# Layer 1 of a two-layer attention block: keys, queries and landmarks of all head pairs first, then each pair's iteration beside two other pairs

## The chip, the cores and the metric

The kernel runs on one core of one Trainium2 chip. The core has a matrix engine (TensorE, PE in the profile; its weight loads are listed apart as PEld), three engines for element-wise work (VectorE or DVE, ScalarE or ACT, GpSimd or POOL), and queues for DMAs, of which this kernel uses that of SyncE (SP) for nearly all and POOL's for a few. The metric is the device time of one execution in microseconds (us). Everything is computed in fp32; each fp32 matmul of the program appears in the profile as two instructions.

## What is computed

The input x has 2 batch items of 512 channels and 64 x 32 = 2048 tokens. There are two layers; both have 8 heads of 64 channels, which the kernel takes two at a time as a "pair", so a batch item has 4 pairs.

Layer 0 is a full softmax attention over 2048 tokens, with an embedding added to keys and queries, an output projection, and the residual.

Layer 1 is a Nyström attention on the normalised tokens xn, and after it a linear feed-forward on the normalised sum:

```
q, k, v = split(xn @ Wqkv);  q = q / 8
qL, kL  = mean of q and of k over each run of 8 tokens       # 256 landmarks
attn1 = softmax(q  @ kL.T)      # 2048 x 256
attn2 = softmax(qL @ kL.T)      # 256 x 256
attn3 = softmax(qL @ k.T)       # 256 x 2048
out   = attn1 @ (pinv(attn2) @ (attn3 @ v)) + conv(v)   # 33 taps along the tokens
t     = t + out @ Wout + bout
t     = t + (norm(t) @ w_lora.T) @ W.T
```

pinv is 6 steps of an iteration that starts from attn2.T divided by (largest row sum times largest column sum) over all heads and both batch items. So every landmark matrix has to exist before the first iteration can start.

## The kernel before

Everything is one program for one core. PE, DVE, ACT and POOL run their instructions in the order in which the Python code emits them; DMA issues on SP are placed by the framework's scheduler, which may put them ahead of their place in the code as soon as the buffer is free. Matmuls write PSUM, which has 8 banks of 128 x 512 fp32. A helper such as `bank` (line 723) hands out a buffer of a pool with a tag; a tag with n buffers is handed out in turn, and who gets one waits until the last user of that buffer is through.

Interleaving is written by hand with generators. A generator emits a unit of work up to each `yield`; `advance(gens, n)` (line 765) takes n units from a list of generators. So "beside" means: units of one thing are emitted between steps of another, on the same engines.

PSUM in before: tag `pp` with 2 banks (`bank`), tag `sc` with 2 double banks (`scores_bank`, 128 x 2 x 512), and `av0`, `av1` with one bank each, which `values_bank` hands out alternately.

The order of the work:

- Layer 0: `attention0` (line 1030) for each of 8 pairs, with the projections of the next pair beside it. Beside the last of them (batch item 1, pair 3) run `landmarks_beside(0)` (line 1244), which computes landmarks and attn2 of batch item 0 from token sums of xn that the normalisation has stored, and keys and values of layer 1's first pair.
- The output projection and normalisation of batch item 1 (`out0`, `norm0_steps`, from line 1805), with attn3, queries and convolution of layer 1's first pair beside them.
- `landmarks_staged` (line 1268): landmarks, attn2 and its Gram matrix for the 4 pairs of batch item 1. `Landmarks.project` (line 1178) multiplies the pooled tokens by the weights (line 1183), `attend` (line 1192) makes attn2, `gram` (line 1221) its product with itself. `start_scale` (line 1297) reduces the scale.
- For each of 8 pairs, batch item 0 first (line 1850): attn3 and queries, `iteration_start`, convolution, then `pinv` (line 1533), then `attn1` (line 1614) with the values of the next pair beside it. Keys of the next pair come at the end of `pinv`. The output part of batch item 0 (`finish1_units`, line 1716) is the only filler inside `pinv`, from the fifth pair on.
- The output part of batch item 1 at the end.

The iteration works on symmetric 256 x 256 matrices M[h] and R[h] of both heads h, with 64 more columns for the vectors. `square` (line 1544) multiplies a matrix by itself in two blocks, `flip` (line 1527) transposes one block into its mirror place: a PE transpose into PSUM and an ACT copy back. One step of the iteration is: `square(M[h])` for both heads (PE tile `pa`), DVE combinations (line 1553), `square(R[h])` for both heads (`pb`), DVE combinations again.

Of the kernel before, what the change touches and what calls it, by code (L numbers as in the profile page):

```python
# [10 lines left out]
F32 = mybir.dt.float32  # L11
# [5 lines left out]
P = 128  # L17
# [5 lines left out]
TB = 512  # L23
# [638 lines left out]
def fast_path(  # L662
# [32 lines left out]

    nc = tc.nc
# [3 lines left out]
    ps = ctx.enter_context(tc.tile_pool(name="ps1", bufs=2, space=bass.MemoryType.PSUM))  # L700
# [12 lines left out]
    pooled_d = dram.tile([B, P, KC, LM], F32, name="pooled_fd")  # L713
    mT_d = dram.tile([P, KC, C], F32, name="mT_fd")
    X_d = dram.tile([B, NPAIR, P, 4, LM], F32, name="X_fd")
# [13 lines left out]
    def values_bank(name):  # L729

        i = values_bank.made % 2
        values_bank.made += 1
        return ps.tile([P, 512], F32, tag=f"av{i}", name=name, bufs=1)

    values_bank.made = 0
# [233 lines left out]
    def norm0_steps(b, t, xb, xn, part, pooled=None):  # L969


        toks = slice(t * TB, (t + 1) * TB)
        name = f"n0_{b}_{t}"
        squares = lambda: (xb[:, :2, :], xb[:, 2:, :])
        for rstd in statistics(xb, xn, part, name, squares, lambda: deviation(name)):
            yield
        nc.vector.reciprocal(rstd, rstd)
        wide = rstd.unsqueeze(1).to_broadcast([P, 2, TB])
        other = nc.vector if t == NTB - 1 else nc.gpsimd
        other.tensor_tensor(xn[:, 2:, :], xn[:, 2:, :], wide, ALU.mult)  # L980
        nc.vector.tensor_tensor(xn[:, :2, :], xn[:, :2, :], wide, ALU.mult)
        nc.gpsimd.dma_start(chunked(xh_d[b])[:, :, toks], xn)
        yield
        n = TB // POOL
        landmarks = slice(t * n, (t + 1) * n)
        if pooled is None:
            pl = small.tile([P, KC, n], F32, tag="pl", name=f"pl_{name}", bufs=1)
            parts = [(pl, xn)]
        else:
            parts = [(pooled[i][:, :, landmarks], xn[:, 2 * i : 2 * i + 2, :]) for i in range(2)]  # L990
        for to, of in parts:
            nc.vector.tensor_reduce(to, of.rearrange("p k (m l) -> p k m l", l=POOL), AX.X, ALU.add)
        if pooled is None:
            nc.sync.dma_start(pooled_d[b][:, :, landmarks], pl)
        yield
# [3 lines left out]
    def finish0_units(b, oTs, outs_done):  # L999
        last = None  # L1000
        for t in range(NTB):
# [10 lines left out]
            if last:  # L1012
                yield from gap()
                next(last)
# [11 lines left out]
        next(last)  # L1026
        yield from gap(2)
# [136 lines left out]
    def load_w(w, hp, n):  # L1164
        for j in range(n):
            lo = j * HEADS * D + hp * P
            nc.sync.dma_start(w[:, :, j, :], chunked(wqkv[:, lo : lo + P]))

    class Landmarks:

        def __init__(self, b, hp, pooled, w, X):
            self.b, self.hp, self.i = b, hp, b * NPAIR + hp
            self.pooled, self.w, self.X = pooled, w, X
            load_w(w, hp, 2)

        def project(self):
            L = row_of(f"L_{self.i}").rearrange("p (j m) -> p j m", j=2)
            lp = bank(f"lp_{self.i}")  # L1180
            for j in range(2):
                for k in range(KC):
                    nc.tensor.matmul(
                        lp[:, j * LM : (j + 1) * LM], lhsT=self.w[:, k, j, :], rhs=self.pooled[k // 2][:, k % 2, :],
                        start=k == 0, stop=k == KC - 1,
                    )
            for j in range(2):
                nc.scalar.mul(L[:, j, :], lp[:, j * LM : (j + 1) * LM], (D**-0.5 if j == 0 else 1.0) / POOL)
            nc.sync.dma_start(L_d[self.b, self.hp], L)
            self.L = L  # L1190

        def attend(self):
            i, L = self.i, self.L
            X = self.X = self.X()
            rs = small.tile([P, 4], F32, tag="rs2", name=f"rs2_{i}")
            for h in range(2):
                nc.gpsimd.memset(X[h][:, :, LM:], 1.0)
            for h in range(2):
                rows_h = slice(h * D, (h + 1) * D)
                sc = bank(f"sc2_{i}_{h}")  # L1200
                for t in range(2):
                    nc.tensor.matmul(
                        sc[:, t * LM : (t + 1) * LM],
                        lhsT=L[rows_h, 0, t * P : (t + 1) * P],
                        rhs=L[rows_h, 1, :],
                        start=True,
                        stop=True,
                    )
                nc.scalar.activation(X[h][:, :, :LM], sc.rearrange("p (t n) -> p t n", n=LM), AF.Exp)
            for h in range(2):  # L1210
                two = slice(2 * h, 2 * h + 2)
                x_h = X[h][:, :, :LM]
                nc.vector.tensor_reduce(rs[:, two], x_h, AX.X, ALU.add)
                nc.vector.reciprocal(rs[:, two], rs[:, two])
                nc.vector.tensor_tensor(
                    x_h, x_h, rs[:, two].unsqueeze(2).to_broadcast([P, 2, LM]), ALU.mult
                )
                nc.sync.dma_start(X_d[self.b, self.hp][:, two], x_h)
                nc.vector.tensor_reduce(rsum[:, i, two], x_h, AX.X, ALU.add)

        def gram(self, h):

            i, X = self.i, self.X
            a = zpool.tile([P, 2, LM + D], F32, tag=f"R{h}", name=f"A0_{i}_{h}")
            for t in range(2):
                pr = bank(f"pr_{i}_{h}_{t}")
                cols = slice(t * P, LM + 1)
                for k in range(2):
                    nc.tensor.matmul(
                        pr[:, cols],  # L1230
                        lhsT=X[h][:, k, t * P : (t + 1) * P],
                        rhs=X[h][:, k, cols],
                        start=k == 0,
                        stop=k == 1,
                    )
                nc.scalar.copy(a[:, t, cols], pr[:, cols])
                nc.sync.dma_start(A_d[self.b, self.hp, h][:, t, t * P :], a[:, t, t * P : LM])
            nc.vector.tensor_copy(csum[:, i, 2 * h : 2 * h + 2], a[:, :, LM])

    def pooled_tiles(b):  # L1240
        tiles = [zpool.tile([P, 2, LM + D], F32, tag=f"M{i}", name=f"pooled_{b}_{i}") for i in range(2)]
        return [tile[:, :, :LM] for tile in tiles]

    def landmarks_beside(b):

        pooled = pooled_tiles(b)
        for i in range(2):
            nc.sync.dma_start(pooled[i], pooled_d[b][:, 2 * i : 2 * i + 2])
        for hp in range(NPAIR):
            w = wpool1.tile([P, KC, 3, P], F32, tag="w", name=f"wL_{b}_{hp}")  # L1250
            lm = Landmarks(
                b, hp, pooled, w,
                lambda: [
# [789 lines left out]
```

## Time and profile before

| | |
|---|---|
| median of 3 runs | 2875.84 us (2872.44 to 2879.71) |
| the profiled execution's own time | 2879.97 us |
| its span, first to last instruction | 2878.2 us |
| PE busy | 2787.5 us (97%) |
| DVE busy | 1746.6 us (61%) |
| ACT busy | 870.6 us (30%) |
| POOL busy | 262.5 us (9%) |
| DMA | 103.59 MB, mean 36 GB/s |

Times inside the span count from its start. Layer 0's attention ends near 1460 us, the landmarks of batch item 1 near 1640 us, and the eight iterations with their surroundings near 2750 us. "Busy" of PE is modelled: ends of matmuls are not observed, so a busy PE isn't necessarily at its peak. The clock column of a stretch is the mean share of full TensorE clock that was granted in it. A row of the table of groups has the line, the engine, the operation, output and inputs, the shape, the count, then busy time and mean duration of one in ns, then the idle time of the engine before these instructions and what ended it.

### The profile page before, as it was taken

To read this page: it belongs to the slowest core of one execution; us is meant where nothing else is said; L and a number is where in the kernel's file an instruction comes from. 1 tells how busy PE (TensorE), PEld (TensorE's weight loads), DVE (VectorE), ACT (ScalarE), POOL (GpSimd) and SP (SyncE) were. 2 spreads that over 40 slices of the span, in tenths; PEclk is the share of its full clock that TensorE was granted. 3 is DMA by queue.
4 is the path that set the end of the run, shared out by engine and by line. 5 is a ranking of instruction groups with operands and counts; after the bars stand their busy time and mean duration, and the time that the engine had idled before them with its cause. 6 is when DMAs were issued, how large, how long until landed. Compare 5 with 4: busy or idle time off the path is not lost. (4 is left out here: it accounts for less than half of the span.)

```text
span 2878.2 us, 39302 instructions
## 1 busy us (share of the span) xinstructions
PE 2787.5 (97%) x16834; PEld 1384.1 (48%) x16834; DVE 1746.6 (61%) x1955; ACT 870.6 (30%) x1158; POOL 262.5 (9%) x160
## 2 busy tenths in 40 slices
PE   8999999999999999999999999999999988999999
PEld 4343443434343343344444756566656534565633
DVE  3869788765667857657558364535445544454475
ACT  1344434433243344444331221212121301222110
POOL 1101011010101100100002010101010100001010
PEclk9999999999999999999999999999999999999999
DMA  3000000101012100022024200002000010000021
GB/s 114 1 5 1 5 1 1 60 15 45 27 47 73 51 1 1 1 79 79 28 74 167 87 14 17 17 20 83 6 23 32 17 53 34 10 19 13 1 72 47
DMA packets 78152, 103.59 MB, mean 36 GB/s; under 512 B 8320, under 2 KB 48016, under 8 KB 77712
## 3 DMA queue, kind: packets, MB, share of 16 engines
q1 hardware_dynamic: 73472, 84.16, 9.1%
q0 software_dynamic: 4416, 16.79, 1.5%
q8 instruction: 134, 2.20, 0.3%
q14 instruction: 50, 0.41, 0.0%
q10 hardware_dynamic: 80, 0.03, 0.0%
HBM read 64.13 MB, written 36.84 MB: 35 GB/s over the span
## 5 line engine op out<-in xcount | busy, mean ns | idle before, releaser
L1060 DVE TENSOR_TENSOR acc_f<-acc_f,p_f 128x1024 f32<-128x1024 f32 x448 | 609.9, 1361 | 239.6 <-ACT p_f L1050 211.3
L1050 ACT ACTIVATE p_f<-sc_f 128x1024 f32<-128x1024 f32 x512 | 497.0, 1022 | 574.0 <-PE sc_f L1042 566.5
L1042 PE MATMUL sc_f<-q_f,k_f 64*64 64x512 f32 x4096 | 494.2, 598 | 3.3 <-ACT p_f L1050 3.3
L1072 PE MATMUL av_f<-p_f,v_f 64*64 64x512 f32 x4096 | 484.0, 589 | 0.0
L1072 PEld LDWEIGHTS av_f<-p_f,v_f 64*64 64x64 f32 x4096 | 156.6, 133 | 282.9 <-issue 282.9
L1042 PEld LDWEIGHTS sc_f<-q_f,k_f 64*64 64x64 f32 x4096 | 144.2, 133 | 292.0 <-issue 251.6
L1329 PE MATMUL pp<-xh,w 128*128 128x512 f32 x512 | 234.2, 603 | 5.8 <-ACT q L1335 2.3
L1540 PE MATMUL pa<-M 128*128 128x192 f32 (+1 forms) x640 | 156.9, 381 | 0.0
L1645 POOL TENSOR_TENSOR o<-o,rinv 128x512 f32<-128x512 f32 x32 | 58.3, 1821 | 1028.2 <-DVE rinv L1643 1025.5
L1540 PE MATMUL pb<-R 128*128 128x192 f32 (+1 forms) x640 | 151.2, 379 | 0.0
L1329 PEld LDWEIGHTS pp<-xh,w 128*128 128x128 f32 x512 | 93.5, 191 | 117.4 <-issue 102.4
L1091 POOL TENSOR_TENSOR q_f<-q_f,rinv_f 128x512 f32<-128x512 f32 x32 | 67.5, 2109 | 850.1 <-DVE rinv_f L1090 850.1
L1642 DVE RECIPROCAL rinv<-rs 128x512 f32<-128x512 f32 x32 | 107.4, 3356 | 56.2 <-PE rs L1638 56.2
L909 PEld LDWEIGHTS vp<-w,xh 128*128 128x128 f32 x1024 | 118.4, 194 | 25.8 <-ACT p L1610 14.6
L909 PE MATMUL vp<-w,xh 128*128 128x128 f32 x1024 | 124.0, 280 | 3.3 <-ACT R L1516 3.3
L1540 PEld LDWEIGHTS pb<-R 128*128 128x128 f32 x640 | 113.9, 193 | 25.5 <-issue 0.5
L1540 PEld LDWEIGHTS pa<-M 128*128 128x128 f32 x640 | 111.5, 196 | 25.0 <-issue 2.0
L909 PEld LDWEIGHTS vp_f<-wv_f,x 128*128 128x128 f32 x1024 | 115.6, 192 | 12.7 <-issue 10.2
L924 PE MATMUL yp_f<-q_f,wo_f 128*128 128x512 f32 x256 | 118.8, 619 | 2.4 <-DVE rinv_f L1090 2.4
L864 PE MATMUL pp_q_f<-x,wq_f 128*128 128x512 f32 x256 | 118.4, 616 | 1.1 <-DVE ft_q_f L850 0.7
L909 PE MATMUL vp_f<-wv_f,x 128*128 128x128 f32 x1024 | 118.5, 276 | 0.0
L924 PE MATMUL yp_g<-o,wo_f 128*128 128x512 f32 x256 | 113.4, 596 | 4.0 <-DVE xb_g L931 2.2
(193 smaller groups left out, 2973.6 us busy)
## 6 DMA issues: line engine op xcount, KB each, us to landing
x<-in_x_dram SPq DMA_DIRECT2D x8, 1024.0 KB, 5.3
xr_f<-in_x_dram SPq DMA_DIRECT2D x8, 1024.0 KB, 5.0
x_fd<-xr_f POOLq DMA_DIRECT2D x8, 1024.0 KB, 4.7
xh_fd<-xn_f POOLq DMA_DIRECT2D x8, 1024.0 KB, 4.6
xh<-xh_fd SPq DMA_DIRECT2D x8, 1024.0 KB, 5.0
xb_g<-x_fd SPq DMA_DIRECT2D x32, 256.0 KB, 4.6
out_dram<-xb_g SPq DMA_DIRECT2D x32, 256.0 KB, 2.3
w<-in_wqkv_dram SPq DMA_DIRECT2D x24, 256.0 KB, 3.7
```

The costliest lines, as they stand in the source:

```text
L864: nc.tensor.matmul(pp, lhsT=w_sb[kind][:, k, cols], rhs=xbs[t][:, k, :], start=k == 0, stop=k == KC - 1)
L909: nc.tensor.matmul(vp[:, j * P : (j + 1) * P], lhsT=xb[:, k, j * P : (j + 1) * P], rhs=w_of(k), start=k == 0, stop=k == KC - 1,)
L924: nc.tensor.matmul(yp, lhsT=wo_sb[:, k, m * P : (m + 1) * P], rhs=oTs[k][:, toks], start=k == 0, stop=k == NPAIR - 1,)
L1042: nc.tensor.matmul(sc[r * D : (r + 1) * D, h, :], lhsT=hd.k[rows, lo : lo + D], rhs=hd.q[rows, t * TB : (t + 1) * TB], start=True, stop=True,)
L1050: nc.scalar.activation(p, sc, AF.Exp, scale=D**-0.5)
L1060: nc.vector.tensor_tensor(acc, first if c == 1 else acc, p, ALU.add)
L1072: nc.tensor.matmul(av[r][half, :], lhsT=hd.v[keys, c, half], rhs=pp[keys, h, :], start=c == 0, stop=c == NST - 1,)
L1091: nc.gpsimd.tensor_tensor(o, o, rinv, ALU.mult)
L1329: nc.tensor.matmul(pp, lhsT=self.w[:, k, j, :], rhs=self.xhs[t][:, k, :], start=k == 0, stop=k == KC - 1)
L1540: nc.tensor.matmul(dst, lhsT=lhsT[:, k, t * P : (t + 1) * P], rhs=rhs[:, k, :], start=k == 0, stop=k == 1)
L1642: nc.vector.reciprocal(rinv, rs)
L1645: nc.gpsimd.tensor_tensor(o, o, rinv, ALU.add)
```

## The change

Landmarks no longer come from pooled tokens. All keys and queries of layer 1 are computed first, pair after pair; each projection unit copies its bank with ACT, stores the piece to a DRAM buffer (`k_d`, `q_d`), and DVE reduces it to landmarks and to its largest magnitude. `attend` and `gram` of a pair run as its `front`, beside the projection of the next pair. Later each pair's keys and queries are read back from DRAM.

Then the iterations run, batch item 1 first. Between the steps of `pinv` of pair n there are 17 places called `slot()`. Each takes one unit of attn1 of pair n-1 (`before`) and one unit of `second(n + 1)` (`nexts`): values 4, attn3 5, landmark values 2, start values 2, convolution 4 units; from the fifth pair on also a unit of the output part of batch item 1 in every other slot. Two units of attn1 come ahead of the first slot.

PSUM is handed out anew after the projections: tag `pp` 3 banks, `pr` 2 banks (products of the iteration, one bank each instead of two), `av0` (all flips), `av1` (attn1's values), `av3` (attn3's values). Attention scores of attn1 and attn3 therefore go to two single `pp` banks with two ACT exponentials of 512 columns, where before they went to one double bank with one exponential of 1024. The scaling of M by the start scale moves from POOL to DVE. Outputs of two pairs are parked in DRAM (`o_d`). The pooled sums in `norm0_steps` and the class `Landmarks` with its projection go.

The core of the diff:

```diff
+    def side_bank(i, name):
         return ps.tile([P, 512], F32, tag=f"av{i}", name=name, bufs=1)
+    def product_bank(name):
+        return ps.tile([P, 512], F32, tag="pr", name=name, bufs=2)
...
+        def keys_and_queries(self, pool, tag, xhs, after=lambda t: None):
...
+            for t in range(NTB):
+                toks, marks = slice(t * TB, (t + 1) * TB), slice(t * TB // POOL, (t + 1) * TB // POOL)
+                for j, dst, dst_d in ((1, k, k_d), (0, q, q_d)):
+                    pp = bank(f"pp{j}_{self.name}_{t}")
+                    for c in range(KC):
+                        nc.tensor.matmul(
+                            pp, lhsT=self.w[j][:, c, :], rhs=xhs[t][:, c, :], start=c == 0, stop=c == KC - 1
+                        )
+                    nc.scalar.copy(dst[:, toks], pp)
+                    nc.sync.dma_start(dst_d[self.b, self.hp][:, toks], dst[:, toks])
+                    nc.vector.tensor_reduce(
+                        self.L[j][:, marks], dst[:, toks].rearrange("p (m l) -> p m l", l=POOL), AX.X, ALU.add
+                    )
+                    nc.vector.tensor_reduce(
+                        big[:, j, t : t + 1], dst[:, toks], AX.X, ALU.max, apply_absolute_value=True
+                    )
+                    if t == NTB - 1:
+                        L = self.L[j]
+                        nc.vector.tensor_scalar(L, L, (1.0, D**-0.5)[j == 0] / POOL, None, ALU.mult)
+                        nc.sync.dma_start(L_d[self.b, self.hp][:, j, :], L)
+                    yield
...
+        def front(self):
+            self.attend()
+            yield 3
             for h in range(2):
+                self.gram(h)
+                yield 0
...
         def attn3(self):
...
+                scs = [bank(f"sc3_{self.name}_{s}_{h}") for h in range(2)]
...
+                for h in range(2):
+                    nc.scalar.activation(p[:, h, :], scs[h], AF.Exp)
...
         def landmarks_values(self):
...
+            rinv = self.acc3[0]
+            yT = rinv[:, LM:]
+            nc.vector.reciprocal(rinv[:, :LM], rs[:, :LM])
+            nc.vector.tensor_tensor(yT, self.av3[:, :LM], rinv[:, :LM], ALU.mult)
+            yield
+            tp = bank(f"tp_{self.name}")
+            for t in range(2):
+                nc.tensor.transpose(tp[:, t * P : (t + 1) * P], yT[:, t * P : (t + 1) * P], ident)
...
         def flip(self, X, name):
-            tp = values_bank(f"tp_{name}_{self.name}")
+            tp = side_bank(0, f"tp_{name}_{self.name}")
             nc.tensor.transpose(tp[:, :P], X[:, 0, P:LM], ident)
             nc.scalar.copy(X[:, 1, :P], tp[:, :P])
...
+            self.flip(M[0], "M0")
+            flip = M[1], "M1"
             for it in range(PINV_ITERS - 1):
                 for h in range(2):
                     pr = square(M[h], f"pa_{it}_{h}_{self.name}", flip)
...
-                advance(gens, n_fill)
+                slot()
                 for h in range(2):
                     pr = square(R[h], f"pb_{it}_{h}_{self.name}", flip)
...
-                advance(gens, n_fill)
+                slot()
                 self.flip(M[0], f"M0_{it}")
                 flip = M[1], f"M1_{it}"
+            slot()
             self.flip(*flip)
...
+                self.product_transposed(wide, src, M, f"{i}")
+                slot()
+                tp = self.into_rows(wide, side_bank(0, f"tp_{i}_{self.name}"))
...
+                slot()
...
+        def attn1(self):
             for t in range(NTB):
...
+                    scs = [bank(f"sc1_{self.name}_{t}_{j}_{h}") for h in range(2)]
...
+                    for h, sc in enumerate(scs):
+                        nc.scalar.activation(p[:, h, :], sc, AF.Exp, scale=D**-0.5)
                     yield
+                acc = apool.tile([P, 2, 512], F32, tag="acc", name=f"acc1_{self.name}_{t}")
+                nc.vector.tensor_tensor(acc, *ps_, ALU.add)
+                av = side_bank(1, f"av1_{self.name}_{t}")
...
+                yield
                 rs = bank(f"rs1_{self.name}_{t}")
...
                 nc.vector.reciprocal(rinv, rs)
+                nc.vector.tensor_tensor(rinv, av, rinv, ALU.mult)
+                nc.gpsimd.tensor_tensor(self.o[:, toks], self.o[:, toks], rinv, ALU.add)
+                yield
...
+    def beside(main, other):
+        for n in main:
+            yield
+            for _ in range(n):
+                if next(other, other) is other:
+                    break
+                yield
...
+    banks.close()
+    ps = ctx.enter_context(tc.tile_pool(name="ps2", bufs=3, space=bass.MemoryType.PSUM))
...
+    def slot():
+        nonlocal made
+        advance(before)
+        advance(nexts)
+        made += 1
+        if finish and (made % 2 or n == len(todo) - 1):
+            advance(finish)
...
+    for n, pair in enumerate(todo):
+        if n + 1 < len(todo):
+            todo[n + 1].prefetch()
+            nexts.append(second(n + 1))
...
+        pair.iteration_start()
         if n:
+            advance(before, 2)
...
+        pair.pinv(slot)
+        while before or nexts:
+            advance(before)
+            advance(nexts)
+        before.append(pair.attn1())
```

## The prediction

> **What bounds the kernel now.** I read the page's busy times, then the table by stretch for where PE is not full, then the groups by shape for what a piece costs, then the chain of waits inside an iteration, then the timeline at the widest hole.
>
> ```profile
> span 2878.2 us, 39302 instructions
> PE 2787.5 (97%) x16834; PEld 1384.1 (48%) x16834; DVE 1746.6 (61%) x1955; ACT 870.6 (30%) x1158; POOL 262.5 (9%) x160
> ```
>
> PE carries the kernel, so only two things can change the time: the sum of PE's work, and holes in it. The table by stretch (length; busy PE, PEld, DVE, ACT, POOL with counts; PE clock; DMA share, GB/s) shows the holes: the staged landmarks of batch item 1, an ordinary iteration with its surroundings, and the output part of batch item 0 where no other work was left.
>
> ```profile
> 1560.00:1640.00 80.00, 71.78 (x377) 51.94 (x376) 42.84 (x66) 19.77 (x44) 8.01 (x16) 0.93 0.37 123
> 1874.20:2004.80 130.60, 128.98 (x722) 79.53 (x724) 63.42 (x99) 30.33 (x55) 11.98 (x8) 1.00 0.13 41
> 2300.00:2420.00 120.00, 97.53 (x296) 43.25 (x294) 49.74 (x54) 10.20 (x15) 0.00 (x0) 0.89 0.15 51
> ```
>
> An iteration has 1.6 us of holes in 130.6. The chain of waits (start, length, what) shows why:
>
> ```profile
> 1894.17 2.81 PE pb L1540 x12
> 1901.87 2.81 PE pb L1540 x12
> 1909.57 2.81 PE pb L1540 x12
> ```
>
> One step of `pinv` follows the other every 7.7 us with no filler at all, and the chain stays on PE. Putting other work between the steps has next to nothing to cover.
>
> ```profile
> L1183 PE MATMUL lp<-pooled,wL 128*128 128x256 f32 x128 | 31.0, 399 | 1.2 <-ACT X L1209 1.2
> L1642 DVE RECIPROCAL rinv<-rs 128x512 f32<-128x512 f32 x32 | 107.4, 3356 | 56.2 <-PE rs L1638 56.2
> L1466 DVE RECIPROCAL acc<-rs 128x256 f32<-128x256 f32 x8 | 14.0, 1756 | 5.2 <-PE rs L1457 5.2
> L1420 ACT ACTIVATE p<-sc 128x1024 f32<-128x1024 f32 x64 | 62.4, 1024 | 87.8 <-PE sc L1412 86.1 <-DVE acc L1440 1.6 <-ACT p L1420 0.2
> L1209 ACT ACTIVATE X<-sc 128x512 f32<-128x512 f32 x16 | 9.0, 597 | 7.5 <-issue 3.4 <-PE sc L1202 3.4 <-DMA wL<-in_wqkv_dram 0.5
> ```
>
> These five rows are prices: a removed projection, the two slow DVE operations, and exponentials of 1024 and 512 columns. The timeline at 2348 us prices a hole:
>
> ```profile
> 2347.87 1.12 PE L946 MATMUL mean_g<-xn_g,mean_w 128*128 128x512 f32 x2 [2.83 <-DVE xn_g L943]
> 2355.12 2.05 PE L959 MATMUL var_g<-sq_g,mean_w 128*128 128x512 f32 x2 [6.13 <-DVE sq_g L956]
> ```
>
> Two matmuls of one size take 1.12 us here, and 2.05 after 6 us of idleness.
>
> **What the Trainium skill says.** "TensorE: Matmul & The Clock Gate", Part 1: the clock falls to half after an idle window of some 3.4 us, a window that runs freely. The trace agrees, by the two rows above and the clock column (0.89 at 2300:2420); holes near 2 us are often enough. "TensorE: Matmul & The Clock Gate", Part 2: matmuls stay in program order, only weight loads are pulled ahead, so one waiting matmul holds all behind it. At 2378.80 PE stood 1.45 us for a bank that DVE had not read, with 16 matmuls ready behind. "ScalarE: Activation LUTs", What ACT_TABLE_LOAD costs: about 0.19 us fixed and 0.83 ns per element; for 512 and 1024 columns 0.61 and 1.04, measured 0.597 and 1.024. So two half exponentials cost 1.19 for 1.02.
>
> **What goes.** (1) Landmark projections: 31.0 us of PE (L1183); all else PE does is still done. (2) Staged landmarks: 80 - 71.8 = 8 us of holes and 0.07 x 80 = 6 of clock, 14. Their matmuls move beside projections. (3) The bare output part: 120 - 97.5 = 22.5, plus about half of the clock deficit of 13 (the rest falls into the holes), less 2 that is ordinary: 27. (4) The iterations' own holes, 8 x 1.6 = 13, which the waits below replace. Sum 85.
>
> **What comes at no cost.** ACT takes all projection copies (0.59 us per unit of 3.44 of PE), DVE two reductions (0.69 each by L1219's shape, 1.4 per unit); PE's unit hides both, uncovered they would be 2 us in each of 64 units. M's scaling moves to DVE (six short operations, about 1.5 us by L1137's 0.42 for 512 columns) behind two attn1 units of 2.1 us. Stores and reloads of k and q (33.6 MB), xn again (4.2) and parked outputs (4.2) add 42 MB to 104, in a kernel whose DMA share in an iteration is 0.06 to 0.13; weights have three buffers, and the landmark, key and query reloads have an iteration's lead.
>
> **What comes at a cost, and what is late next.**
>
> A. `attend` is emitted straight after the last query unit of the same pair. Its matmuls need ACT's copy (0.59), two DVE reductions (1.37), the scaling (0.25, half of L1137's 0.42) and four hand-overs (0.06 each): 2.4 us, with the next pair's projection queued behind on PE. Seven pairs (the first is long ready), and about 1.2 each for the clock: 25.
>
> B. The first `second` runs almost bare: attn3's bank and exponential waits 5.3, then sums, 1.76 + 0.42 on DVE, a load of X (3.5 to landing before) and copies: 12.
>
> C. Per iteration, with attn1 and `second` at their slots counted out:
>  - attn3's scores: two steps want four of three `pp` banks, so the second half-bank waits for the first exponential, 0.65; four groups, 2.6.
>  - All flips share `av0`. After a slot behind `pb`, M0's copy stands behind two exponentials of 0.6; M1's transpose waits for it while PE has 0.75 of its own: 0.85 in slots 6 and 8, 0.25 behind a values copy in slots 2 and 4: 2.2.
>  - Slot 10 holds attn1's third sums and attn3's sums: DVE then has 3.36 + 0.69 + 1.76 + 0.42 = 6.2. The transposes of slot 11 need the last. PE has 1.08 (L1457) + a flip 0.1 + a score unit 1.06 (L1602, 67.9/64): 2.2. Hole 4.1 with hand-overs, and 1.7 of clock: 5.8.
>  - X is loaded into the buffer that those transposes free: about 0.5 beyond PE's cover.
>  - Slot 14's reciprocal and product (4.05) stand before the tail's combination (0.57); PE has two convolution units and transposes, 2.9: 1.8.
>  - At the start two score units come back to back: 0.65 for a bank, 0.8 for a flip behind exponentials: 1.4.
>
>  Together 14.3. Six iterations have both neighbours: 86. The first and last, with one neighbour, 5 each: 10. Output units in later slots cover about 11. So 85.
>
> D. More changes between 64-row and 128-row matmuls, some 0.2 to 0.3 us each, about three or four more per pair: 7. E. The new PSUM pool, a mean without cover, and the last pair's attn1 with few units left beside it: 5.
>
> Sum of costs 25 + 12 + 85 + 7 + 5 = 134. Net +49 on the profiled execution's own 2879.97 (1.8 above its span): 2929. It stood 4.1 above the median of the runs, so the median comes to **2925 us**, 1.7% slower.
>
> The unknown terms from both sides: C's waits from 1 us a pair (the queues drain while PE is on longer pieces) to 20 (each hole adds its own half-clock window); A from 0 (DVE is quicker than PE comes) to 7 x 4.1 = 29; late loads from 0 to 6 us an iteration. I take C near its worked value since every wait in it is in program order.
>
> **Rivals.** *The cover holds, faster.* Mechanism: C's queues on DVE and ACT empty in time. DVE is busy 63 of 130 us and ACT 30, which speaks for it; that both work in order, and that slot 10 puts two reciprocals in one place, against. With 1 us a pair (7 over seven pairs) costs are 25 + 12 + 7 + 7 + 5 = 56, net -29: 2847. It decides where C is under (85 - 49)/7 = 5.1 us a pair. *It comes out level*: C near 5 us, 2876. *SP's queue becomes late.* 64 stores and the reloads join one issuing queue; X at slot 12 has little lead, and a load behind a store that waits for ACT comes later still. 4 us and 1.7 of clock in seven iterations add 40: 2965. The load of xb_g that held PE at 2378 speaks for it, the scheduler's early issues against. That interleaving doesn't happen I exclude, since the order is written out.
>
> **How the numbers follow.** The likeliest case, 2885 to 2960, has 0.55; the cover holds (below 2867) 0.17; level (within 0.3%, about what a measurement can tell here: 2867 to 2884) 0.08; SP late (above 2960) 0.20. Faster 0.17, same 0.08, slower 0.55 + 0.20 = 0.75. The range for 8 in 10 reaches into both neighbours: 2850 to 2985.
>
> **What would show it.** Right: no `lp` row; PE idle before attn2's scores of 2.4 us, seven times, released by DVE; transposes of attn3's result waiting 4 us for DVE; flips of M1 waiting for ACT; a clock column under 1 in iterations; the bare output holes gone. Wrong: iterations of about 105 us with PE holes below 5 us, or PE waiting for DMA landings of X, k or q. Most likely to fail is C's slot 10, if output or other units fall between, and A, if the clock takes more or less.

## The result, and the profile after

The changed kernel takes 2946.64 us, the median of 4 runs (2943.27 to 2949.19), beside 2874.4 us of the kernel before on the same chip: ratio 1.0248, 95% interval 1.0228 to 1.0267. It is 2.5% slower. The forecast was 2925 us in a range of 2850 to 2985. In the profiled executions the span went from 2878.2 to 2941.3 us, so 63 us where the prediction's sum said 49. Between the medians it is 72: the profiled execution of the kernel before was longer than its four runs, that of the changed kernel the shortest of its four.

From the page's first lines after the change:

```profile
span 2941.3 us, 39554 instructions
PE 2804.2 (95%) x16706; PEld 1376.3 (47%) x16706; DVE 1770.1 (60%) x2133; ACT 896.6 (30%) x1310; POOL 221.5 (8%) x130
```

There are 128 matmuls fewer, and PE is still busy 16.7 us longer. Idle time of PE (span less busy) went from 90.7 to 137.1 us, 46.4 more. The mean granted clock fell from 0.989 to 0.984, which is 31.7 us of deficit before (0.011 x 2878.2) and 47.1 after (0.016 x 2941.3), 15.4 more. With 31.0 us of landmark projections gone, 63.1 - 46.4 - 15.4 + 31.0 = 32.3 us are left, at least, since part of the clock's deficit falls into the holes: PE was busy longer with the same matmuls, without a hole that the view shows. Three kinds of loss; the forecast had put the third, its part D, at 7.

The table by stretch of the changed kernel (length; busy PE, PEld, DVE, ACT, POOL with counts; PE clock; DMA share, GB/s): the projections with `attend` among them, the bare first `second`, three plain iterations, and the stretch where the last pair's attn1 stands beside the output part.

```profile
1510.00:1740.00 230.00, 210.01 (x600) 102.99 (x600) 123.58 (x227) 52.41 (x97) 9.39 (x18) 0.98 0.47 157
1740.00:1785.00 45.00, 37.98 (x285) 28.91 (x286) 14.59 (x31) 13.43 (x27) 0.37 (x1) 0.89 0.30 96
1870.00:1986.00 116.00, 108.41 (x654) 69.33 (x652) 57.38 (x102) 29.99 (x69) 4.24 (x4) 0.97 0.10 33
1986.00:2103.00 117.00, 109.72 (x659) 71.54 (x661) 57.14 (x101) 29.62 (x68) 5.73 (x5) 0.97 0.20 68
2103.00:2218.00 115.00, 108.07 (x656) 69.55 (x652) 56.68 (x99) 29.61 (x68) 4.88 (x4) 0.97 0.10 33
2720.00:2805.00 85.00, 67.75 (x179) 23.95 (x178) 51.52 (x45) 18.67 (x28) 6.65 (x5) 0.92 0.22 74
```

An iteration took 130.6 us before, with eight units of keys and queries (3.44 us each, 27.5) in it. Without them 103.1 are left (102.2, if each unit is counted from its start to the next start, 3.56 us); it now takes 116 to 117, at clock 0.97 instead of 1.00. The table of PE's waits (engine, line, waited for: us in total, times, longest) names who is late:

```profile
PE tp L1395 <- DVE acc L1391: 14.8, 6, 2.5
PE sc L1252 <- DVE most L1226: 13.7, 6, 2.3
...
PE wp L1480 <- DVE R L1519: 8.4, 5, 1.7
PE var_g L969 <- DVE sq_g L966: 8.1, 1, 8.1
PE sc L1334 <- ACT p L1343: 7.8, 27, 0.7
PE tp_R L1495 <- DVE R L1519: 7.4, 6, 4.7
...
PE wp_y L1480 <- DMA X<-X_fd: 3.1, 1, 3.1
```

The top two are slot 10 and `attend`. Apart from a wait at the very start that the kernel before has too (8.6 and 8.5 us), DMA is there with one wait of 3.1 us, in the first `second` only: SP's queue did not hold the iterations.

The chain of waits in a plain iteration, where one step of `pinv` used to follow the other on PE alone, now leaves PE at slot 10:

```profile
2078.21 2.81 PE pb L1505 x12
2081.01 1.03 PE rs L1593 x4
...
2082.14 3.37 DVE rinv L1597
...
2085.53 0.69 DVE rinv L1598
2086.22 1.68 DVE acc L1390
...
2087.92 0.44 DVE acc L1391
...
2088.49 0.53 PE tp L1395 x2
```

From the end of attn1's sums to the start of the transposes the chain is on DVE: 3.37 + 0.69 + 1.68 + 0.44 = 6.2 us, which is the prediction's sum for this place. The timeline at three holes (start, length, what, idle before and its releaser) has `attend`, the transposes and the tail's product:

```profile
1597.61 1.14 PE L1252 MATMUL sc<-L,L 64*128 64x256 f32 x8 [2.28 <-DVE most L1226]
...
2088.49 0.53 PE L1395 MATMUL tp<-ident,acc 128*128 128x128 f32 x2 [2.48 <-DVE acc L1391]
...
2102.70 1.19 PE L1480 MATMUL wp<-M,R 128*64 128x256 f32 x8 [1.69 <-DVE R L1519]
```

### The profile page after: what moved, and what is told of

The parts are those of the page before. It is cut to its first block, busy times and chain, and to the rows that moved or that the text cites. A ratio compares the mean times of both kernels' runs of the same rounds, so it can differ in the third digit from the quotient of the medians.

```text
span 2941.3 us, 39554 instructions
## 1 busy us (share of the span) xinstructions
PE 2804.2 (95%) x16706; PEld 1376.3 (47%) x16706; DVE 1770.1 (60%) x2133; ACT 896.6 (30%) x1310; POOL 221.5 (8%) x130
## 4 chain that ended last, share of the span: by engine, by line
PE 82%; DVE 13%; ACT 2%; issue 2%; DMA 1%; POOL 0%; DVEq 0%; ACTq 0%; POOLq 0%; SPq 0%
PE sc_f L1035 12%; PE av_f L1065 12%; PE pp L1209 8%; PE pb L1505 5%; PE vp L919 4%; PE pa L1505 4%; PE vp_f L919 4%; PE pp_k_f L874 4%; DVE acc_f L1053 4%; PE yp_g L934 4%; PE fp_g L1653 4%; PE yp_f L934 3%; PE pp_q_f L874 3%; DVE rinv L1597 3%; PE sc L1573 2%; PE sc L1334 2%
## 5 line engine op out<-in xcount | busy, mean ns | idle before, releaser
L1519 DVE SCALAR_TENSOR_TENSOR M<-M,pb 128x320 f32<-128x320 f32 (+1 forms) x160 | 59.8, 416 | 137.2 <-PE pb L1505 137.2
L1519 DVE SCALAR_TENSOR_TENSOR R<-M,pa 128x320 f32<-128x320 f32 (+1 forms) x160 | 60.1, 417 | 129.7 <-PE pa L1505 129.7
L1597 DVE RECIPROCAL rinv<-rs 128x512 f32<-128x512 f32 x32 | 107.4, 3357 | 26.6 <-PE rs L1593 26.0
L919 PEld LDWEIGHTS vp_f<-wv_f,x 128*128 128x128 f32 x1024 | 115.6, 192 | 12.7 <-issue 11.0
L1599 POOL TENSOR_TENSOR o<-o,rinv 128x512 f32<-128x512 f32 x32 | 42.9, 1341 | 1003.6 <-DVE rinv L1598 1003.6
```

The costliest lines, as they stand in the source:

```text
L919: nc.tensor.matmul(vp[:, j * P : (j + 1) * P], lhsT=xb[:, k, j * P : (j + 1) * P], rhs=w_of(k), start=k == 0, stop=k == KC - 1,)
L1519: nc.vector.scalar_tensor_tensor(out, m, scale, pr, ALU.mult, ALU.subtract)
L1597: nc.vector.reciprocal(rinv, rs)
```

## The experiments

The theory under test: the loss is a list of separate waits behind short in-order queues (A at `attend`; C's bank wait, slot 10 and slot 14; E at the end), and each goes when its cover is given. The main rival: the iteration is bound elsewhere, and a hole closed in one place opens in the next. The medians below are to be held against 2946.6 us (changed kernel) and 2874 to 2876 (kernel before); "a plain iteration" is the mean distance from one repetition of attn1's score unit in slot 11 to the next, over three, which is 116.5 us in the changed kernel. Two limits: the changed kernel itself was run four times (2943.3 to 2949.2), so a difference of a few microseconds from it says little; and the two runs whose edits leave a plain iteration as it was (at `attend`, and in the last iteration) have 115.6 us in it, so differences of under 1 us there say nothing while half clock falls into it (at full clock, as in the later runs, it repeats to 0.1 us).

### One unit ahead of each `attend`

```diff
+            next(units)
+            yield
             yield from beside(last.front(), units)
```

The same at the two other places that call `front`. 

> Edit of the changed kernel: the next pair's first projection (or value) unit is emitted ahead of each attend, so 3.4 us of PE work stands between the last query unit and the landmark scores. Theory (each attend really holds PE 2.3 us, and some of the holes also cost clock): the seven holes before the landmark scores go, 16 us, with up to 8 us of clock, so 2922 to 2931 us. Rival (the wait only moves: the projections behind then wait for ACT, which has the exponentials first): 2944 to 2949, with new holes of the same sum before projections or grams.

Measured: 2926.85 us, ratio to before 1.0183 (1.0166 to 1.0200), so 19.8 us less than the changed kernel. The row of groups of the landmark scores has no idle time left:

```profile
L1252 PE MATMUL sc<-L,L 64*128 64x256 f32 x64 | 11.6, 402 | 0.0
```

Before the edit it had 16.0 us of idleness. The next projection waits three times, 2.7 and 0.8 us for ACT's exponentials and 0.7 for its copy, where the changed kernel has two such waits of 0.65. In the trace the holes of PE fell by 18.9 us: 16.0 here, less these 2.9, and 6.3 in the normalisation just before the first `attend`, of which some 2 also go in runs whose edits do not come near it. So A is confirmed as a wait that ends with cover, at about 20 us where 25 were forecast, give or take a few; the wait was 2.28 (forecast 2.4), but half clock came only behind three of the seven holes.

### A convolution unit between attn3's sums and the transposes

```diff
-        yield from pair.landmarks_values()
-        yield from pair.start_values()
...
-        yield from pair.convolution(o)
+        conv = pair.convolution(o)
+        landmarks = pair.landmarks_values()
+        next(landmarks)
+        yield
+        next(conv)
+        yield
+        yield from landmarks
+        yield from pair.start_values()
+        yield from conv
```

> Edit of the changed kernel: one convolution unit is put between attn3's sums (slot 10) and the transposes of its result, which so come one slot later; no work is added. Theory (the hole is two DVE reciprocals in a row, 6.2 us, against 2.2 us of PE): seven holes of about 3.2 us go, and the half clock of 3.4 or 6.8 us after each gives 1.7 to 3.4 more, so 35 to 45 us less: 2902 to 2912. Rival (only the place moves: the transposes or the load of X, the product behind it or the next start become late in its place): within 6 us of 2946.6, with a hole of 3 us or more per iteration elsewhere. A hole at X's load of up to 1 us would not decide it.

Measured: 2966.82 us, ratio 1.0325 (1.0306 to 1.0344): 20 us slower than the changed kernel, outside both expectations. The waits of PE in this kernel:

```profile
PE wp_y L1480 <- DMA X<-X_fd: 22.5, 8, 3.4
PE sc L1252 <- DVE most L1226: 13.7, 6, 2.3
PE wp L1480 <- DVE R L1519: 13.4, 6, 2.6
```

The transposes wait only once more, 1.3 us in all, as the theory said. In their place PE waits for X. The timeline of the DMA issues, and PE's at X's product in a plain iteration and in the last one, tell why:

```profile
2085.83 0.53 SPq L1402 DMA_DIRECT2D X<-X_fd  x1
2094.13 0.33 SPq L1452 DMA_DIRECT2D q<-q_fd  x1
2094.56 0.52 SPq L1402 DMA_DIRECT2D X<-X_fd  x1
...
2099.83 1.98 PE L1480 MATMUL wp_y<-X,Y 128*64 128x256 f32 x8 [3.31 <-DMA X<-X_fd]
...
2609.71 1.08 PE L1480 MATMUL wp_y<-X,Y 128*64 128x256 f32 x8 [1.12 <-DMA X<-X_fd]
```

The half of X whose buffer is free with the sums goes out at 2085.83. The other half goes into the buffer that holds attn3's result until the transposes have read it, so it goes out 8.7 us later, behind the 1 MB load of the next queries, and PE needs it at 2096.5. It arrives 3.3 us after that.

Two things differ from the changed kernel. There, too, this half goes out only with the transposes, but 3.6 us of PE work stand between them and X's product; one slot later it is 2.1. And there it lands 2.9 us after its issue, ahead of the queries' load; here it takes 5.1, behind it. The last iteration has no such load just ahead: X lands in 3.0 us, and PE waits 1.1. So some 2 of the 3.3 us go with the load ahead and the rest with the shorter cover. That is read from the trace; no run changed one of the two alone. It is the prediction's "X is loaded into the buffer that those transposes free" (there 0.5 us), at the price that the edit itself gave it.

### The same, with X's buffers freed early

```diff
-            rinv = self.acc3[0]
+            rinv = row_of(f"rinv3_{self.name}")
```

The allocation and load of X (five lines) also move ahead of the `yield` that stands before the transposes. 

> Edit of the changed kernel: the convolution unit between attn3's sums and the transposes, as in the run that became slower; besides, attn3's result is kept in a buffer of its own, so that X's buffers come free with the sums and X is loaded a slot earlier. Theory (the reciprocals' hole did go there, and X, released late and behind the load of the next queries, took its place): no wait for the reciprocals and none for X, 2900 to 2920. Rival (the hole of the transposes is not what cost there, or X is late for another reason, such as traffic): 2940 or more, with PE still waiting for a landing of X.

Measured: 2924.18 us, ratio 1.0166 (1.0149 to 1.0183): 22.4 us less than the changed kernel and 42.6 less than the run above. A plain iteration takes 112.6 us. Neither the transposes nor X are waited for in an iteration:

```profile
2084.45 0.44 PE L1400 MATMUL tp<-ident,rinv 128*128 128x128 f32 x2
...
2086.81 1.03 PE L1480 MATMUL wp_y<-X,Y 128*64 128x256 f32 x8
...
2094.03 1.51 PE L1480 MATMUL wp<-M,R 128*64 128x256 f32 x5 [2.51 <-DVE R L1519]
```

The last line is the next one late: the tail's product now waits 2.51 us (1.69 before the edit), because the cover ahead of it went to slot 11. In all these waits grew by 5.0 us, which is what the 22 lack to the low end of the expected range, 27. So the hole on DVE is the cause at slot 10, the load of X stands in the way of closing it, and slot 14 is late next.

### attn1's last reciprocal one slot later

```diff
+                if t == NTB - 1:
+                    yield
                 rinv = row_of(f"rinv1_{self.name}_{t}")
```

> Edit of the changed kernel: the reciprocal and product of attn1's last sums come one slot after their matmuls, so behind the tail's combination on DVE and no longer ahead of it. Theory (the combination waits behind 4.05 us of DVE, so its product waits 1.7 us, seven times, with half clock behind two of them): 12 to 18 less, 2929 to 2935. Rival (the same 4 us on DVE then stand ahead of the next combination): within 5 us of 2946.6, with the wait at the next product.

Measured: 2934.11 us, ratio 1.0205 (1.0188 to 1.0222): 12.5 less. A plain iteration takes 113.5 us, 3.0 less, and the tail's product no longer waits there. About half of the whole gain was not foreseen: at the end, the 8.1 us that PE stood for the variance of the first output block became 1.6 us, since that block's squares no longer stand behind attn1's last reciprocal. On the other side 4.8 us of waits came in three other rows (for the means, and for ACT's copies of the convolution).

### attn3's scores and value products by step

```diff
-                for s, p in pending:
-                    values(s, p)
-                pending = [(s, scores(s)) for s in steps[i : i + 2]]
+                made = []
+                for j in range(2):
+                    for s, p in pending[j : j + 1]:
+                        values(s, p)
+                    made += [(s, scores(s)) for s in steps[i + j : i + j + 1]]
+                pending = made
```

> Edit of the changed kernel: in attn3, value products of the group before and scores of this one alternate by step, where both value products came first. Theory (the second step's second half-bank waits for the first exponential, 0.5 to 1 us, four times a pair): eight pairs by 2.5 us, 20 less, of which the longer string of switches between shapes may take back up to 6: 2926 to 2934. Rival (the wait is on ACT's throughput, not on the order, since four exponentials of 0.6 us follow each other anyway): within 5 us of 2946.6.

Measured: 2937.94 us, ratio 1.0220 (1.0202 to 1.0237): 8.7 less, between the two expectations. A plain iteration loses 1.55 us where 2.5 were forecast (0.7, if held against the 115.6 above). The groups of attn3's scores in this kernel:

```profile
L1334 PE MATMUL sc<-L,k 64*128 64x256 f32 x512 | 78.2, 402 | 4.1 <-ACT p L1343 2.0 <-DVE rinv L1600 2.0
```

Their idle time fell from 12.5 to 4.1 us and their busy time from 85.7 to 78.2. That is 15.9, of which 7.5 were no hole before: a wait for a half bank can hide in the busy time, as the run with all four edits shows below. 5.0 of it came back in two other rows: PE's waits for R's combination went from 7.4 to 10.0 us and those for M's flips from 2.1 to 4.5.

### The kernel before with short landmark projections

In the kernel before, the landmark projections sum one block of 128 channels of four, so a part of the computation is left out.

```diff
-                for k in range(KC):
+                for k in range(1):
...
-                        start=k == 0, stop=k == KC - 1,
+                        start=True, stop=True,
```

> Edit of the kernel before, which leaves out part of the computation: the landmark projections sum one block of 128 channels where there are four. It removes 96 of their 128 matmuls, three quarters of the row's 31.0 us. Theory of the prediction's step (1) (this work is on the path in full): 23 us less, 2849 to 2856. Rival (part of it runs in the shadow of holes in the staged landmarks and beside attn1): 5 to 15 us less, 2860 to 2870; then the change's removal was worth less than 31 us.

Measured: 2853.99 us, ratio 0.9929 (0.9909 to 0.9949), 20.0 us less, with 15 to 26 in the interval. The row of `lp` fell from 31.0 to 8.9 us. Step (1) holds in kind. Scaled to the whole row it is 26.7 (20.0 x 4 / 3) against 31.0; the interval takes in both.

### Bare steps

```diff
-    def slot():
+    def turn():
...
+    def slot():
+        nonlocal passed
+        passed += 1
+        if passed > 10:
+            turn()
...
         while before or nexts:
-            advance(before)
-            advance(nexts)
+            turn()
```

> Edit of the changed kernel: the ten slots of the five pinv steps emit nothing; attn1 of the other pair and the other's values, attn3 and convolution alternate in the tail's seven slots and after them. No work is added or left out. Theory (a bare step has no hole, so the slots had nothing to cover; they only add banks and flips that wait and switches of shape, some 5 us a pair): the five steps take 7.7 us each with PE full, and the time is 2946.6 less up to 35, so 2910 to 2945, with the slot-10 hole of attn3's result still there. Rival (the slots did cover something, and back to back attn1 and attn3 units wait for exponentials and sums in the other's absence): 2960 to 3000.

Measured: 2956.44 us, ratio 1.0281 (1.0264 to 1.0298): 9.8 slower than the changed kernel, between the two expectations. A plain iteration takes 115.8 us, no less than the 115.6 above. The steps themselves have no hole: from one step's first flip to the next, 2116.66 to 2124.65 to 2132.53, it is 8.0 and 7.9 us. So the prediction's "next to nothing to cover" holds. But the holes of the other pairs' units stay, and three plain iterations have clock 0.96 where the units in slots have 0.97. The first iteration, which has one neighbour, is 7.9 us longer. In the whole run PE waits 8.9 us for X (3.1 in the changed kernel), once more 2.4 for the transposes, and 9.3 for a variance (8.1).

### Fewer output units in the last iteration

```diff
-        if finish and (made % 2 or n == len(todo) - 1):
+        if finish and made % 2:
```

> Edit of the changed kernel: in the last iteration the output units of batch item 1 come at every second slot as before it, instead of at every slot, so some 8 units are left to stand beside the last pair's attn1. Theory (the prediction's step E, sized 5, cost some 20 because that attn1 stands nearly alone): the holes of 3.6, 1.7 and 8.1 us there shrink, 8 to 20 us less, 2927 to 2939. Rival (the last iteration loses as much cover as the last attn1 gains): 2942 to 2950, with longer holes in the last iteration.

Measured: 2961.55 us, ratio 1.0296 (1.0279 to 1.0313): 15 slower; worse than the rival said. PE in the last iteration and after it:

```profile
2659.18 0.30 PE L1495 MATMUL tp_R<-ident,R 128*128 128x128 f32 x1 [3.28 <-DVE R L1519]
2686.25 0.48 PE L1495 MATMUL tp_M<-ident,M 128*128 128x128 f32 x1 [5.47 <-ACT M L1496]
2702.27 2.16 PE L1480 MATMUL wp<-M,R 128*64 128x256 f32 x8 [6.38 <-DVE R L1519]
2759.52 2.05 PE L956 MATMUL mean_g<-xn_g,mean_w 128*128 128x512 f32 x2 [6.09 <-DVE xn_g L953]
```

The last iteration needs the cover as much as the last attn1 does: attn1's reciprocals of 3.36 us stand ahead of the steps' own combinations, and with nothing on PE beside them each shows. So at the end the cover is short in all, and this move of it did not help.

### The four edits together

> The changed kernel with four edits together: the unit ahead of each attend, attn3's scores and value products by step, the convolution unit between sums and transposes with X's buffers freed, and attn1's last reciprocal one slot later. Theory (separate terms of one sum): the single gains of 19.8, 8.7, 22.4 and 12.5 us add to 63, so 2883, and the wait of 2.5 us before the tail's product that the third left is removed by the fourth, up to 8 more: 2875 to 2885, level with the kernel before or up to 0.4% slower. Rival (they are one stall seen at different places, and the last one stays): 2895 or more, with a hole of 2 us or more in each iteration.

Measured: 2875.13 us, 13 runs, against 2875.8; ratio 1.0000 (0.9991 to 1.0008). The whole 2.5% is back. The stretch of one plain iteration in this kernel:

```profile
1939.35:2047.38 108.03, 105.41 (x657) 68.28 (x656) 57.87 (x101) 29.46 (x68) 5.38 (x4) 1.00 0.22 74
```

It takes 108.0 us where the changed kernel has 116.5, 8.5 less; the three edits that touch it gave 1.55 + 3.0 + 3.9 = 8.5 singly (each known to about 1). In the whole kernel 71.5 us came back, and the single gains add to 63. So the rival of one stall that only moves falls; the terms are separate to within 8 us, and the clock, which is 1.00 again, is part of that.

But level is all that it is. PE is busy 2788.5 us here, as in the kernel before (2787.5), though 31.0 us of projections are gone, and idle 85.7, less than before (90.7). What eats the gain now is the third kind of loss, time of PE without a hole. Most of it lies in the score units. Counted from start to start, less the holes, attn1's take 10.3 us of a plain iteration (8.1 in the kernel before) and attn3's 9.2 (7.7). In the kernel before, the matmuls of the two heads start within 0.01 us of each other in all 64 score units of attn1, and a unit takes 1.0 us. In the changed kernel, and with the four edits, the second head starts late in 19 of the 64, which take 1.5 us or more, mostly 1.9 to 2.3. Here are two units one behind the other, first in the kernel before, then with the four edits (matmuls, and the second head's weight load):

```profile
2736.17 1.99 PE L1602 MATMUL sc<-q,L 64*128 64x512 f32 x8
...
1955.71 2.93 PE L1576 MATMUL sc<-q,L 64*128 64x512 f32 x8
...
1957.52 0.29 PEld L1576 LDWEIGHTS sc<-q,L 64*128 64x128 f32 x2 [0.66 <-ACT p L1581]
```

The second head waits for its single bank until ACT has read it. The first head's matmuls fill that time, so PE shows no hole, but the two no longer run side by side.

### Together, with bare steps in six iterations, and in four

```diff
-        if passed > 10:
+        if passed > 10 or n in (0, len(todo) - 1):
```

> The same four edits, and in the six iterations that have both neighbours the five pinv steps stand bare, with the other pairs' units in the tail and after it. Theory (with the holes gone, half clock no longer takes back what the steps gain by fewer switches and flips, some 2.3 us an iteration by the bare run): 14 us less than the four edits alone, 2860 to 2872, just faster than before. Rival (the units packed together wait for each other's banks and reciprocals, 1 to 3 us an iteration): 2875 to 2895.

Measured: 2890.37 us, ratio 1.0054 (1.0040 to 1.0068). A plain iteration takes 107.4 us, 0.65 less than with units in the slots. That is a net: the iteration has 1.2 us of holes where it had 2.6, and the bare steps go faster, but attn1's score units, which now follow each other, take 12.1 us of the iteration where they took 10.3. The loss lies where output units run: from the same mark on, 123.6 us instead of 119.9 up to the first of them, and 500 instead of 491 from there to the end.

```diff
-        if passed > 10:
+        if passed > 10 or n not in (1, 2, 3, len(todo) - 1):
```

> The four edits, with bare pinv steps only in iterations 1 to 3 and in the last one, and the units in the slots elsewhere. In the run with bare steps in six iterations each plain iteration took 107.4 us in place of 108.0, and the loss came where output units run (iterations 5 and 6); in the run with bare steps in all, the stretch from the last iteration on took some 7 us less than in the changed kernel. Theory (in the last iteration the units' reciprocals stand ahead of the steps' own combinations on DVE, which holds of 4.7 and 2.0 us show): 2 + 7 = 9 us less than the four edits alone, 2862 to 2870, 0.3% faster than before. Rival (the output units left over find less to stand beside): 2873 to 2885.

Measured: 2881.09 us, 21 runs, ratio 1.0021 (1.0014 to 1.0029). The time is where the rival had it. The holes of 4.7 and 2.0 us in the last iteration went, and others of 2.4, 2.6 and 7.6 us came behind it.

### Two flips in one bank, and sums on GpSimd

```diff
-            tp = side_bank(0, f"tp_{name}_{self.name}")
+            i = int(name[1])
+            if i == 0:
+                self.tp = side_bank(0, f"tp_{name}_{self.name}")
+            tp = self.tp[:, i * P : (i + 1) * P]
...
-                        nc.vector.tensor_tensor(self.acc3[h], src, p[:, h, :], ALU.add)
+                        (nc.vector, nc.gpsimd)[h].tensor_tensor(self.acc3[h], src, p[:, h, :], ALU.add)
```

> The four edits of the level kernel and two more: the two flips of a pair of matrices take two halves of one bank, so the second does not wait for the copy of the first; and half of attn3's sums of exponentials go from DVE to GpSimd, which has under 10% of work. Theory (in that kernel's plain iterations PE waits 0.83 us for a combination on DVE behind four such sums, and 0.4 twice for a flip's copy; the second is the prediction's one-bank flip term in C): 1.2 to 2 us an iteration, 8 to 16 in all, 2859 to 2867, 0.3 to 0.5% faster than before. Rival (GpSimd's sums are slower than DVE's and delay attn3's sums or DVE itself; the bank is not what the flips wait for): 2872 to 2885, with new waits for GpSimd.

Measured: 2876.29 us, 13 runs, ratio 1.0005 (0.9996 to 1.0013): no gain. PE's wait for the combination behind the sums (0.83 us an iteration) went. M's second flip still waits 0.46 us for ACT's copy, though it has its own half of the bank. Two plain iterations of three are 0.7 us shorter, and one is 0.6 longer, with a window of half clock in it. The flip term of the prediction is not settled by this: the second flip waits for the first one's copy either way, and no run took that wait away. None of the kernels that compute everything beats the kernel before by more than can be told.

## Why the prediction was right

The sign held, and so did the main mechanism: small in-order waits outweigh what was removed, and most of them were taken away singly. That the sum came so near is in part luck, since C's waits were smaller than forecast and D's loss much larger. The parts, in the prediction's own order:

- **Removed 85.** Step (1), 31.0: three quarters of it measured 20.0 where 23 was expected. Right, perhaps 4 too high. The holes of the staged landmarks (2) and of the bare output part (3) were not tried singly.
- **A, 25.** Seven holes of 2.28 us against 2.4; 19.8 us by the run. The clock term was too large: half clock of 3.4 us followed three holes of seven, 5.1 us in all where 8 were forecast.
- **B, 12.** 7.0 us idle and 0.11 x 45 = 5 of clock in the stretch 1740 to 1785. Right.
- **C with its neighbours, 14.3 less 1.6 of own holes, and 1 of D, so 13.7 an iteration.** Measured 116.5 - 103.1 = 13.4. Right in the sum by luck: C's own waits make some 10 of it, and D the rest. Attn3's bank wait was 0.7 to 1.55 by the run (2.6 forecast), slot 10 3.9 net of what came behind it (5.8), the tail 3.0 (1.8), each known to about 1. X was put at 0.5 and cost nothing, because 3.6 us of PE work stood ahead of its product. The start's score units and the flips, 3.6 in the forecast, show as some 1.5 in the timeline.
- **D, 7.** The term that was most undersized, and its reason, changes between 64-row and 128-row matmuls, is not what the traces show. With the four edits in, an iteration is still 108.0 - 103.1 = 4.9 us above the kernel before's without its projections: 1.0 more of holes (2.6 against 1.6), at full clock, and 3.9 of PE time without holes, or 27 in seven iterations, where D had 1 a pair. Of these, 3.8 lie in the score units of attn1 and attn3, where the second head waits for its single bank and the two heads no longer run side by side. So most of it is C's half-bank wait, in a form that C did not price. No run took it away at attn1; at attn3 the reordered steps, which lessened the same wait, also took 7.5 us off the busy time.
- **E, 5.** Mis-sized. The stretch 2720 to 2805 has 17.3 us of idleness and 0.08 x 85 = 6.8 of clock. Not all of it is new: from the last product of `pinv` to the end the changed kernel has 26.0 and 8.9, the kernel before 12.3 and 1.5, so some 21 more. The step spoke of "few units left beside it"; what it left out is that an attn1 unit brings 4.05 us of DVE at each fourth slot, ahead of the output part's own short operations. The late reciprocal took 6.5 us of it away and thereby showed the mechanism for that part.

A was 5 too high and E some 16 to 19 too low, which would make most of the 14 us between 49 and 63; how the rest is shared out stays open, since (2) and (3) were not tried. The rival *the cover holds* falls: it needed C under 5.1 us. *SP's queue becomes late* was not what happened in the changed kernel, as the table of waits shows; the first convolution run met part of its mechanism, with X behind the queries' load.

## What to carry to other kernels

Interleaving two streams pays where one has holes for the other to fill; here the host stream had 1.6 us of them in 130 us, and each guest brought waits of its own. When one puts units into another's slots, list for every slot what each in-order queue already holds, and put two units between a long operation on a slow queue and its reader. When an edit moves the work that frees a buffer, the load into that buffer moves with it and may fall behind another, so free the buffer in the same edit; the two convolution runs differ by 43 us in that alone. And when two matmuls run side by side, as those of two heads do here, see that both their banks come free together, as the double bank of the kernel before does: a wait of the second shows in no idle column, only in the busy time of the group.

## What had not been expected of the hardware

- In each trace all windows of half clock begin on one grid of 3.413 us, and they last 3.4 us or a multiple of it. Whether a hole is followed by one goes with how much of it falls into one cell of that grid: of seven equal holes of 2.28 us at `attend`, the three that were followed by half clock had 1.96, 2.21 and 2.27 us of idleness in one cell (two of them with a second hole of 0.65 close behind), the four others 1.23 to 1.88. In all fourteen traces, behind the start-up, no cell with 2.0 us of idleness or more went without half clock after it. Less was enough at times: at slot 10, where a hole of 0.69 and one of 2.48 us lie 1.1 us of work apart, half clock followed in all five iterations that end on it, twice with only 1.0 and 1.1 us in the cell.
- Two matmuls of 64 rows, one of each head, start within 0.01 us of each other and a score unit of both takes 1.0 us; where the second starts late, it takes 1.5 to 3.1.
- GpSimd takes 1.36 us for one of attn3's sums over 512 columns, which DVE does in 0.75 (in that run 0.83 for its own half of them).
- With a 1 MB load one place ahead on the issuing queue, 256 KB (half of X's 512) landed 5.1 us after their issue; without it just ahead, 3.0.
